# Four graph-attention layers: transposes of features and of layer 1's attention taken from TensorE to VectorE and DRAM

## The chip, the cores and the metric

The kernel runs on one core of a Trainium2 chip. A core has TensorE (PE, matrix products), VectorE (DVE), ScalarE (ACT), GpSimd (POOL) and SyncE (SP), each with a queue of its own that it works off in order, and DMA engines [...]. Here SyncE only issues plain DMAs; GpSimd also issues DMAs that add to what lies at the destination. The metric is the device time of one execution in microseconds, as the median of several runs. A profile belongs to one execution; its span runs from the first instruction to the last.

## What is computed

The input is 128 independent graphs of 128 nodes with 512 features each, all float32, and an integer adjacency matrix per graph. Four layers follow one another, and each adds its result to x:

```python
h = maximum(layernorm(x), 0.0)
x = x + attention_layer(h, adj)     # four different ones
```

Each attention layer forms, for every pair of nodes, a score from one number of the source and one of the destination, passes it through a leaky ReLU, masks it with the adjacency, takes a softmax over the neighbours and averages features with these weights. The layers differ as follows.

- Layer 0: one head; the scores come from h by two vectors that are folded out of the weights; the values are h itself; an ELU at the end.
- Layer 1: two attention layers in a row. The first projects 512 features to 1024 (4 heads of 256), with a bias and an ELU; the second projects 1024 to 512 with one head.
- Layer 2: one head, scores from h by two vectors, values h.
- Layer 3: a projection from 512 to 512 with 8 heads of 64, a ReLU at the end.

## The kernel before

A graph is one tile: its 128 nodes are the 128 partitions, its 512 features lie along the free axis. `graph(b)` runs the four layers for one graph as a Python generator that yields one step at a time. `Scheduler` takes the steps of up to `FLYING` = 10 graphs, estimates for each when its engine, its inputs and its buffers would be free (`Step.estimate` holds the assumed durations), and writes out the one that could start first; ties go by `rank`, which gives each graph a due time. So the order of every engine's queue is fixed when the kernel is built. Buffers come from pools by a tag with a count (`tile_of("ht", 3, ...)`), and a stream waits until one has been given back. Every instruction of the graphs is recorded at one line of the scheduler, L252 in the profile before, and groups are told apart by their tiles.

The parts that the change touches:

- `norm_relu` (mean and variance with `bn_stats` and `bn_aggr` on VectorE, the reciprocal root on GpSimd, the scaled ReLU on ScalarE) makes h. Its columns come from a small pool.
- `transposed` turns 128x128 blocks on TensorE against `ident` into a PSUM bank and copies the bank to SBUF on ScalarE. Layers 1 and 3 need h with features first (`ht`, four blocks), since a product takes its left side with the summed index on the partitions. Layer 1 also turns its four heads of attention weights e (`et`), and the other attentions turn one block each in `attended`.
- `rows_in_dram` takes a few columns, one number per node, turns them on TensorE into rows, copies them on ScalarE to `r` and writes `r` to DRAM. From there they are read back by every partition: into layer 1's e by SyncE, and onto layer 3's `sd` by a GpSimd DMA that adds. The last `LATE` = 5 graphs avoid that for layer 3 and add rows on VectorE from PSUM (`add_rows`).
- `projected` multiplies `ht` with the weights: `w1x` for layer 1 in three parts of 344 columns into `fx` (tag `xl`, two of them), `w2x` for its second half in two parts of 257 columns, `wpx` for layer 3 in two parts of 264.
- In `layer1`, VectorE multiplies e by 1/z before it is turned; after the product with the values, VectorE adds the bias, takes the minimum with 0 over all 1024 columns, ScalarE takes the exponential, and VectorE combines them.
- In `layer3`, two SyncE copies fill `sd` with the mask `m` and its transpose `m3t`, each repeated for 8 heads.
- `setup` loads the weights and folds the attention vectors into them; `load` brings x and adj ahead of use.

float32 products go through TensorE as two records each, a transpose as one.

Of the kernel before, what the change touches and what calls it, by code (L numbers as in the profile page):

```python
# [19 lines left out]
SLOPE = 0.2  # L20
EPS = 1e-5
FLYING = 10
AHEAD = 2
# [19 lines left out]
class Step:  # L43
# [17 lines left out]
    def estimate(self, name, outs, ins, kw):  # L61

        if name == "dma_start":

            rate, busy = (290e3, 0.35) if self.engine == "SP" else (105e3, 1.0)
            self.moves = size(outs[0]) * outs[0].shape[0] * 4 / rate
            return busy, 1.0
        n = max(size(a) for a in outs[:1] + ins)
        if self.engine == "PE":
            if name == "transpose":  # L70
                return 0.109, 0.2
            return 2 * max(0.00084 * size(outs[0]), 0.108), 0.2
        if self.engine == "DVE":
            if name == "bn_stats":
                return 0.6, 0.12
            if name == "bn_aggr":
                return 0.09, 0.12
            per = 1 / 960
            if name == "tensor_scalar" and n >= 256:
                per /= 2  # L80
            return n * per + 0.07, 0.12
        if self.engine == "ACT":
            pointers = sum(isinstance(kw.get(k), bass.AP) for k in ("bias", "scale"))
            busy = n * 0.00081 + 0.105 + (0, 0.075, 0.135)[pointers]
            return busy + 0.1 * ("accum_out" in kw), 0.15
        if self.engine == "POOL":
            if kw.get("op") == ALU.pow or ALU.pow in kw.get("ops", ()):
                return 0.6, 0.1
            return (0.25 if n <= 16 else 0.55 if name == "tensor_scalar" else 1.3), 0.1
        raise ValueError(name)  # L90


class Group(Step):
    def __init__(self, steps):
# [5 lines left out]
        self.delay = steps[-1].delay  # L100

# [34 lines left out]
class Scheduler:  # L136
    def __init__(self):
# [3 lines left out]
        self.moved = 0.0  # L141
# [95 lines left out]
    def issue(self):  # L237
# [17 lines left out]
        if step.moves:  # L255

            self.moved = max(end, self.moved) + step.moves
            end = self.moved + 1.0
# [21 lines left out]
def kernel(  # L280
# [31 lines left out]
    AG = 4 if B % 4 == 0 else 1  # L312

# [44 lines left out]

    w1x = rows_of("w1x", KC, E1 + HF)
# [22 lines left out]

    def setup():
# [12 lines left out]
        for c in range(KC):  # L396
            yield S.dma_start(out=w1x[c][:, E1:], in_=l1_w1[c * P : (c + 1) * P])
# [16 lines left out]
        for c in range(KC):  # L414
            yield S.dma_start(
                out=wpx[c][:, :, E3:],
                in_=l3_wp[c * P : (c + 1) * P].rearrange("p (h k) -> p h k", h=H3),
# [25 lines left out]
    def fold(blocks, vecs, per, to):  # L443
# [4 lines left out]
        for g in range(0, len(blocks), 4):  # L448
# [5 lines left out]
                        lhsT=wt[:, j - g, :],  # L454
# [7 lines left out]
            give_back(wt)  # L462
# [33 lines left out]
    def norm_relu(xt):  # L496

        st6 = column("st6", nc.vector.BN_STATS_DIM)
        yield V.bn_stats(st6, xt)
        mv = column("mv", nc.vector.BN_AGGR_DIM)  # L500
        yield V.bn_aggr(mv, st6)
        ve = column("ve")
        yield G.tensor_scalar(ve, mv[:, 1:2], EPS, None, ALU.add)
        rstd = column("rstd")
        yield G.tensor_tensor(out=rstd, in0=ve, in1=minus_half, op=ALU.pow)
        nmr = column("nmr")
        yield V.scalar_tensor_tensor(nmr, mv[:, 0:1], -1.0, rstd, ALU.mult, ALU.mult)
        h = yield tile_of("h", 4, D)
        yield A.activation(out=h, in_=xt, func=AF.Relu, bias=nmr, scale=rstd)
        return h  # L510
# [18 lines left out]
    def transposed(blocks, tag, bufs):  # L529

        n = len(blocks)
        r = yield tile_of(tag, bufs, n, P)
# [4 lines left out]
        yield A.copy(r.rearrange("p m q -> p (m q)"), pt[:, : n * P])  # L537
        give_back(pt)
        return r

    def rows_in_dram(cols, n):

        r = yield Take(work, [2 * H3, P], "r", 4)
        r = r[:n]
        pt = yield bank()
        yield T.transpose(pt[:n, :P], cols, ident)
        yield A.copy(r, pt[:n, :P])
        give_back(pt)
        d = dram.tile([n, P], F32, tag=f"d{n}", name="d")
        yield S.dma_start(out=d, in_=r)  # L550
        give_back(r)
        return d.rearrange("n q -> (n q)").partition_broadcast(P)

    def spread(cols, n, to):

        d = yield from rows_in_dram(cols, n)
        yield S.dma_start(out=to, in_=d)
# [19 lines left out]
    def added(cols, to, late, rows=None):  # L577
# [4 lines left out]
        if rows is None:  # L582
            rows = yield from rows_in_dram(cols, cols.shape[1])
        yield G.dma_start(out=to, in_=rows, accum_op=ALU.add)

    def attention(own, rows, e, mask, nh, exact=False):

        mx = column(f"mx{nh}", nh)  # L590
# [3 lines left out]
                    out=e[:, j, :],  # L594
# [11 lines left out]
        if rows[0].tensor.name != e.tensor.name:  # L606
            give_back(rows[0])
# [6 lines left out]
        if exact:  # L614
            ef = e.rearrange("p h q -> p (h q)")
            yield V.tensor_scalar(ef, ef, own, None, ALU.add)
            yield V.scalar_tensor_tensor(ef, ef, SLOPE, ef, ALU.mult, ALU.max)
        else:
            for j in range(nh):
                yield A.activation(  # L620
                    out=e[:, j, :],
                    in_=e[:, j, :],
# [4 lines left out]
        for j in range(nh):  # L627
            yield A.activation(
                out=e[:, j, :],
                in_=e[:, j, :],  # L630
# [8 lines left out]
    def attended(own, other, mask, values, exact=False):  # L639

        e = yield tile_of("e0", 3, 1, P)
        pb = yield bank()
        yield T.transpose(pb[:, :P], other.to_broadcast([P, P]), ident)
        rz = yield from attention(own, [pb[:, :P]], e, mask, 1, exact)
        et = yield from transposed([e[:, 0, :]], "et0", 3)
        give_back(e)
        pa = yield bank()
        yield T.matmul(pa, lhsT=et[:, 0, :], rhs=values, start=True, stop=True)
# [3 lines left out]
    def projected(lhs, n_k, w, parts, to, beside=None, plus=None):  # L652
# [4 lines left out]
        for i in range(parts):  # L657
            lo = i * width
            pm = yield bank()
            for g in range(0, n_k, 4):  # L660
# [4 lines left out]
                            lhsT=lhs[:, c, :],  # L665
# [41 lines left out]
    def layer1(xt, mask):  # L707
        h = yield from norm_relu(xt)
        ht = yield from transposed(blocks_of(h), "ht", 3)
        give_back(h)  # L710
        yield Until("w1")
        fx = yield tile_of("xl", 2, E1 + HF)
        e = yield tile_of("e1", 3, H1, P)
        rows = e.rearrange("p h q -> p (h q)")
        fork = yield from projected(
            ht, KC, w1x, 3, columns(fx, 3), lambda: spread(fx[:, :H1], H1, rows)
        )
        give_back(ht)
        xl = fx[:, E1:]
        yield Join(fork)  # L720
        rz = yield from attention(fx[:, H1:E1], [e[:, j, :] for j in range(H1)], e, mask, H1)
        yield V.tensor_tensor(e, e, rz.unsqueeze(2).to_broadcast([P, H1, P]), ALU.mult)
        et = yield from transposed([e[:, j, :] for j in range(H1)], "et1", 3)
        give_back(e)
        y = yield tile_of("y1", 2, FC, P)
        for g in range(0, FC, 4):
# [6 lines left out]
                        rhs=et[:, c * P // F1, :],  # L733
# [5 lines left out]
            )  # L739
            yield V.tensor_tensor(  # L740
                y[:, g : g + 4, :],
# [5 lines left out]
        give_back(fx, et)  # L747
        yf = y.rearrange("p c q -> p (c q)")

        t = yield tile_of("t1", 1, HF)  # L750
        yield V.tensor_scalar(t, yf, 0.0, None, ALU.min)
        yield A.activation(out=t, in_=t, func=AF.Exp)
        yield V.scalar_tensor_tensor(yf, t, -1.0, yf, ALU.add, ALU.max)
        give_back(t)
# [3 lines left out]
        yield from projected(y, FC, w2x, 2, columns(gx, 2), plus=columns(b2, 2))  # L758
# [18 lines left out]
    def layer3(xt, mask, mask_t, late):  # L777
# [3 lines left out]
        ht = yield from transposed(blocks_of(h), "ht", 3)  # L781
# [8 lines left out]
        for to, m in (d, mask), (e, mask_t):  # L790
            yield S.dma_start(out=to, in_=m.unsqueeze(1).to_broadcast([P, H3, P]))
            give_back(m)
# [8 lines left out]
        give_back(ht)  # L801
# [12 lines left out]
        fork = None if late else (yield Fork(rows_in_dram(mx, H3)))  # L814
# [60 lines left out]
    def graph(b):  # L875
# [9 lines left out]
        m3t = yield tile_of("m3t", FLYING, P)  # L885
        m1 = yield tile_of("m1", FLYING, P)
# [6 lines left out]
        yield from layer1(xt, m1)  # L893
# [7 lines left out]
        yield from layer3(xt, m3, m3t, b >= B - LATE)  # L901
# [65 lines left out]
```

## Time and profile before

| What | Before |
|---|---|
| Median of three runs | 3410.93 us (3409.13 to 3411.11) |
| The profiled execution | 3414.4 us |
| Its span | 3412.6 us |
| Mean granted TensorE clock | 0.991 |
| VectorE busy | 2617.3 us, 77% |
| ScalarE busy | 2316.5 us, 68% |
| GpSimd busy | 871.6 us, 26% |
| Moved by DMA | 450.33 MB, mean 132 GB/s |

A line of a group reads: line of the code, engine, operation, output<-inputs by tile name (buffer numbers left out), shape, count; then busy time and mean duration of one in ns; then how long the engine was idle just before such instructions, and what ended most of that. Busy time of an engine counts overlapping instructions once, so the groups of an engine whose instructions overlap add up to more than its total. `PEld` is TensorE's loading of weights, which overlaps its products. `SPq` and `POOLq` are the queues that issue DMAs; issuing isn't counted as busy.

### The profile page before, as it was taken

How to read it: one execution, taken by the hardware profiler on the slowest of the kernel's cores; microseconds unless marked ns; L12 is line 12 of the kernel's file. 1: busy time of each engine (PE TensorE's matmuls, PEld its weight loads, DVE VectorE, ACT ScalarE, POOL GpSimd, SP SyncE). 2: the span in 40 equal slices, each digit the busy share in tenths (PEclk: the TensorE clock that was granted, in tenths of full speed). 3: DMA queues.
4: the chain of work that ended last, by engine and by line, in shares of the span. 5: the costliest groups of instructions: out<-in, count | busy, mean ns of one | idle time of the engine just before them, and what ended most of it. 6: DMA issues, size and time to landing. Idle time of an engine off the chain costs nothing.

```text
span 3412.6 us, 56516 instructions
## 1 busy us (share of the span) xinstructions
PE 3381.6 (99%) x17118; PEld 2650.2 (78%) x17118; DVE 2617.3 (77%) x9296; ACT 2316.5 (68%) x6661; POOL 871.6 (26%) x1791
## 2 busy tenths in 40 slices
PE   8999999999999999999999999999999999999998
PEld 5777777777777777777777777777777777777787
DVE  6777777777778777777777787777787777777766
ACT  4667676677677667666767766776776676667764
POOL 1222322222222222222222222222222222222221
PEclk7999999999999999999999999999999999999998
DMA  5155555555556556555655555565565555556553
GB/s 151 45 125 127 139 139 132 131 142 138 131 126 151 129 132 145 132 128 140 143 130 132 133 144 133 138 142 128 123 151 134 134 138 135 131 131 143 131 126 97
DMA packets 392879, 450.33 MB, mean 132 GB/s; under 512 B 27128, under 2 KB 309120, under 8 KB 376832
## 3 DMA queue, kind: packets, MB, share of 16 engines
q0 software_dynamic: 35424, 193.48, 29.3%
q1 hardware_dynamic: 352976, 253.23, 25.4%
q8 instruction: 137, 2.24, 0.3%
q14 instruction: 166, 1.36, 0.1%
q10 hardware_dynamic: 4176, 0.02, 0.1%
HBM read 277.11 MB, written 35.33 MB: 92 GB/s over the span
## 4 chain that ended last, share of the span: by engine, by line
PE 98%; ACT 1%; DVE 1%; issue 0%; DMA 0%; POOL 0%; ACTq 0%; POOLq 0%; DVEq 0%
PE bank L252 98%; DVE sd L252 0%; ACT ht L252 0%; DMA a<-in_L_gnn_a_dram 0%; ACT h L252 0%; ACT sd L252 0%; ACT e L252 0%; DMA at<-in_adj_dram 0%; POOL rstd L252 0%; DVE st L252 0%; DVE products L252 0%; DVE xt L252 0%; DVE e L252 0%; POOL ve L252 0%; DVE mx L252 0%
## 5 line engine op out<-in xcount | busy, mean ns | idle before, releaser
L252 PE MATMUL bank<-w2x,y 128*128 128x257 f32 x4096 | 975.2, 381 | 0.0
L252 PE MATMUL bank<-w1x,ht 128*128 128x344 f32 x3072 | 954.3, 454 | 1.4 <-ACT ht L252 1.4
L252 PEld LDWEIGHTS bank<-w2x,y 128*128 128x128 f32 x4096 | 746.8, 190 | 108.3 <-issue 16.7
L252 PEld LDWEIGHTS bank<-w1x,ht 128*128 128x128 f32 x3072 | 572.2, 191 | 261.1 <-issue 17.9
L252 ACT ACTIVATE h<-xt,nmr,rstd 128x512 f32<-128x512 f32 x512 | 413.6, 808 | 386.1 <-DVE nmr L252 385.0
L252 PE MATMUL bank<-wpx,ht 128*128 128x264 f32 x2048 | 501.9, 388 | 0.0
L252 POOL TENSOR_SCALAR ve<-mv 128x1 f32<-128x1 f32 x512 | 173.5, 339 | 1095.1 <-DVE mv L252 905.5
L252 PEld LDWEIGHTS bank<-wpx,ht 128*128 128x128 f32 x2048 | 381.1, 191 | 87.4 <-DVE y L252 8.6
L252 ACT ACTIVATE sd<-sd,f 128x128 f32<-128x128 f32 x1024 | 366.2, 392 | 0.0
L252 ACT ACTIVATE e<-e,nm 128x128 f32<-128x128 f32 x896 | 351.4, 396 | 13.8 <-DVE e L252 9.5
L252 DVE BATCH_NORM_STATS2 st<-xt 128x6 f32<-128x512 f32 x512 | 350.7, 685 | 0.0
L252 POOL TENSOR_TENSOR rstd<-ve,minus_half 128x1 f32<-128x1 f32 x512 | 313.7, 613 | 42.0
L252 PEld LDWEIGHTS bank<-x,sd 128*128 128x128 f32 x2048 | 266.1, 194 | 48.2 <-issue 12.2
L252 POOL DMA_DIRECT2D sd<-d x246 | 230.7, 994 | 267.5 <-ACT sd L252 136.7
L252 PEld LDWEIGHTS bank<-et,xl 128*128 128x128 f32 x2048 | 250.3, 192 | 38.4 <-issue 37.5
L252 PE MATMUL bank<-et,xl 128*128 128x128 f32 x2048 | 271.8, 276 | 0.2 <-ACT et L252 0.2
L252 PE MATMUL bank<-x,sd 128*128 128x65 f32 x2048 | 260.1, 271 | 7.2 <-ACT sd L252 7.2
L252 PE MATMUL bank<-h,et 128*128 128x512 f32 x512 | 266.1, 601 | 0.7 <-ACT et L252 0.7
L252 ACT COPY xl<-bank 128x344 f32<-128x344 f32 x384 | 166.7, 434 | 135.0 <-PE bank L252 134.6
L252 DVE TENSOR_TENSOR y<-bank,b 128x512 f32<-128x512 f32 x256 | 176.8, 690 | 81.4 <-PE bank L252 72.9
L252 ACT COPY x<-bank 128x264 f32<-128x264 f32 x256 | 96.0, 375 | 210.1 <-PE bank L252 209.9
L252 DVE SCALAR_TENSOR_TENSOR xt<-bank,rz,xt 128x512 f32<-128x512 f32 x256 | 191.3, 747 | 23.6 <-PE bank L252 23.5
(90 smaller groups left out, 5207.0 us busy)
## 6 DMA issues: line engine op xcount, KB each, us to landing
sd<-d POOLq DMA_DIRECT2D x123, 1024.0 KB, 11.0
sd<-m SPq DMA_DIRECT2D x128, 512.0 KB
sd<-m3t SPq DMA_DIRECT2D x128, 512.0 KB
sd<-d POOLq DMA_DIRECT2D x123, 512.0 KB, 8.3
xt<-in_x_dram SPq DMA_DIRECT2D x128, 256.0 KB
e<-d SPq DMA_DIRECT2D x128, 256.0 KB
out_dram<-xt SPq DMA_DIRECT2D x128, 256.0 KB
at<-in_adj_dram SPq DMA_DIRECT2D x32, 256.0 KB
```

Of the source, the lines that this page charges most:

```text
L252: method(*args, **kw)
```

## The change

Features first without TensorE: `turned` transposes a 128x512 tile on VectorE in place, as 32x32 squares (each square within its 32 partitions and 32 columns), writes it to DRAM in four DMAs, one for each group of 32 partitions, with pieces of 512 bytes, and reads it back in one DMA with 2 KB per partition, so that squares come to the partitions where they belong. For h the columns are dealt: feature (q, k) of the 512 stands at 4q + k, so block k takes every fourth column of `ht`, and the rows of `w1x` and `wpx` are loaded in the same order (`dealt`). For layer 1's e the squares are contiguous; e is laid out with the heads inside groups of 32 columns. The last five graphs (`late`) still use TensorE, with dealt columns.

`rows_in_dram` now turns a 128x32 tile of repeated columns on VectorE and writes it to DRAM in four DMAs, or for layer 1 (`together`) in one, from which e is read with 512-byte pieces.

Layer 1's scaling by 1/z moves from VectorE to ScalarE, one instruction per head. Its ELU goes by halves of 512 columns, with ScalarE's ReLU of -y in place of VectorE's minimum. `m3t` is stored in DRAM in between and is read from there. `norm_relu` keeps its columns in one tile of a pool of six. There are three `xl` tiles, two `et1`, two half-sized `t1`, seven `m1`; `FLYING` is 12, `AHEAD` 1, and the scheduler's DMA estimates are changed, with a separate clock for each issuing queue.

```diff
-FLYING = 10
-AHEAD = 2
+FLYING = 12
+AHEAD = 1
 LATE = 5
...
-            rate, busy = (290e3, 0.35) if self.engine == "SP" else (105e3, 1.0)
+            rate, busy, delay = (280e3, 0.4, 0.5) if self.engine == "SP" else (150e3, 1.0, 2.0)
+            if self.engine == "SP" and max(len(a.shape) for a in outs + ins) > 2:
+                busy = 0.65
...
+    Q = nc.vector.STREAM_SQUARE_SIZE
+    R = P // Q
...
+    def dealt(w):
+        return w.rearrange("(p c) n -> c p n", c=KC)
...
-            yield S.dma_start(out=w1x[c][:, E1:], in_=l1_w1[c * P : (c + 1) * P])
+            yield S.dma_start(out=w1x[c][:, E1:], in_=dealt(l1_w1)[c])
...
+    def turned(t, squares, tag, bufs):
+        yield V.transpose(squares, squares)
+        f = t.shape[1] // R
+        d = dram.tile([R, Q, R, f], F32, tag="turned", name="turned")
+        yield Group(
+            [
+                S.dma_start(
+                    out=d[:, :, r].rearrange("m b f -> b m f"),
+                    in_=t[r * Q : (r + 1) * Q].rearrange("b (m f) -> b m f", m=R),
+                )
+                for r in range(R)
+            ]
+        )
+        to = yield tile_of(tag, bufs, R * f)
+        yield S.dma_start(out=to, in_=d.rearrange("m b r f -> (m b) (r f)"))
+        return to
+
+    def features_first(h, late):
+        if late:
+            blocks = h.rearrange("p (q k) -> p k q", k=KC)
+            return (yield from transposed([blocks[:, k] for k in range(KC)], "ht", 3, True))
+        to = yield from turned(h, h.rearrange("p (m b k) -> p m k b", b=Q, k=KC), "ht", 3)
+        blocks = to.rearrange("p (q k) -> p k q", k=KC)
+        return [blocks[:, k] for k in range(KC)]
+
+    def rows_in_dram(cols, n, together=False):
+        r = yield tile_of("r", 5, Q)
+        yield V.transpose(r, cols)
+        if together:
+            d = dram.tile([R, Q, Q], F32, tag="squares", name="d")
+            yield S.dma_start(out=d.rearrange("c m b -> (c m) b"), in_=r)
+            give_back(r)
+            rows = d[:, :n].rearrange("c m b -> c (m b)")
+            return rows.unsqueeze(0).to_broadcast([P, R, n * Q])
+        d = dram.tile([n, R, Q], F32, tag=f"d{n}", name="d")
+        yield Group(
+            [S.dma_start(out=d[:, c], in_=r[c * Q : c * Q + n]) for c in range(R)]
+        )
         give_back(r)
...
-        ht = yield from transposed(blocks_of(h), "ht", 3)
+        ht = yield from features_first(h, late)
...
-        fx = yield tile_of("xl", 2, E1 + HF)
+        fx = yield tile_of("xl", 3, E1 + HF)
...
-        yield V.tensor_tensor(e, e, rz.unsqueeze(2).to_broadcast([P, H1, P]), ALU.mult)
-        et = yield from transposed([e[:, j, :] for j in range(H1)], "et1", 3)
+        for j in range(H1):
+            yield A.activation(out=heads[j], in_=heads[j], func=AF.Copy, scale=rz[:, j : j + 1])
+        if late:
+            et = yield from transposed(blocks_of(e), "et1", 2)
+        else:
+            to = yield from turned(e, e, "et1", 2)
...
-        t = yield tile_of("t1", 1, HF)
-        yield V.tensor_scalar(t, yf, 0.0, None, ALU.min)
-        yield A.activation(out=t, in_=t, func=AF.Exp)
-        yield V.scalar_tensor_tensor(yf, t, -1.0, yf, ALU.add, ALU.max)
+            t = yield tile_of("t1", 2, 4 * P)
+            yield A.activation(out=t, in_=yg, func=AF.Relu, scale=-1.0)
+            yield A.activation(out=t, in_=t, func=AF.Exp, scale=-1.0)
+            yield V.scalar_tensor_tensor(yg, t, -1.0, yg, ALU.add, ALU.max)
...
+        m3t_far = dram.tile([P, P], F32, tag="m3t", name="m3t_far")
+        yield S.dma_start(out=m3t_far, in_=m3t)
+        give_back(m3t)
+        yield from layer1(xt, m1, b >= B - LATE)
```

## The prediction

> **What bounds the kernel now.** The median is 3410.93 us (3409.13 to 3411.11). The profiled execution took 3414.4 us, 3412.6 of them span, so sums made against the span become a median by adding 1.8 and taking off 3.5. I read busy shares first, then the chain that ended last, then TensorE's groups with shapes kept apart.
>
> ```profile
> PE 3381.6 (99%) x17118; PEld 2650.2 (78%) x17118; DVE 2617.3 (77%) x9296; ACT 2316.5 (68%) x6661; POOL 871.6 (26%) x1791
> ...
> q0 software_dynamic: 35424, 193.48, 29.3%
> q1 hardware_dynamic: 352976, 253.23, 25.4%
> ...
> PE 98%; ACT 1%; DVE 1%; issue 0%; DMA 0%; POOL 0%; ACTq 0%; POOLq 0%; DVEq 0%
> ```
>
> TensorE is both 99% busy and 98% of the chain. In the windows its idle time lies at the ends: 15.5 us in the first 80 us, some 14 in the last 72, about 1 us in the others I read. Only removing TensorE work can shorten this kernel, and only while nothing else takes over. The five groups that the change touches:
>
> ```profile
> L252 PE MATMUL bank<-ident,e 128*128 128x128 f32 x896 | 175.6, 274 | 4.8 <-ACT e L252 4.8
> L252 PE MATMUL bank<-ident,h 128*128 128x128 f32 x1024 | 154.7, 274 | 1.1 <-ACT h L252 1.1
> ...
> L252 PE MATMUL bank<-ident,xl 128*4 128x128 f32 x128 | 34.9, 272 | 0.0
> L252 PE MATMUL bank<-ident,f 128*16 128x128 f32 x123 | 33.5, 273 | 0.0
> L252 PE MATMUL bank<-ident,mx 128*8 128x128 f32 x123 | 33.5, 272 | 0.0
> ```
>
> The 274 ns are a duration, not a price: matmuls overlap. The timeline (start, duration) gives the price as start to start:
>
> ```profile
> 1718.57 0.60 PE L252 MATMUL bank<-ident,h 128*128 128x128 f32 x4
> 1719.00 0.27 PE L252 MATMUL bank<-ident,mx 128*8 128x128 f32 x1
> 1719.11 0.74 PE L252 MATMUL bank<-w1x,ht 128*128 128x344 f32 x2
> ```
>
> Four transposes take 0.43 us and one 0.11, so 0.109 us each, narrow or full. The same reading over 800 us gives 0.289 per 344-column matmul and 0.222 per 264-column one.
>
> The last view is SyncE's own queue. The 1 MB of mask copies fills something: the issue behind them takes 6.52 us instead of its usual 0.36.
>
> ```profile
> 1747.40 0.60 SPq L252 DMA_DIRECT2D sd<-m  x1
> 1748.06 0.95 SPq L252 DMA_DIRECT2D sd<-m3t  x1
> 1749.10 6.52 SPq L252 DMA_DIRECT2D out_dram<-xt  x1
> 1755.66 1.22 SPq L252 DMA_DIRECT2D xt<-in_x_dram  x1
> ```
>
> Before, this hits about one graph in four; the others leave the queue empty for some 13 us after the mask copies.
>
> [...] 128x512 should then cost what other one-element passes cost, 686 ns in this trace; no transpose runs before. [...] The new weight blocks step exactly four; nothing in the trace strides so[...]. [...] SyncE's issue above stalls while POOL's two accumulations also run.
>
> **The change, part by part.**
>
> *TensorE.* The order of instructions, changed against before: transposes of h 1024 to 40, of e 896 to 404, of xl 128 to 0, of f (16 columns) 123 to 0, of mx (8 columns) 123 to 0. That is 1850 fewer, 15 per graph in 123 graphs (the last five keep those of h and layer 1's e). 1850 x 0.109 = 202 us. Nothing is added; other matmuls keep their shapes.
>
> *VectorE.* Removed: e times rz (87.8), the min on y (88.2), the 1024-wide combine (155.9): 332 us. Added: 369 transposes of 128x512 at 0.686 = 253; 256 half-width combines at 0.686 = 176; 374 transposes of 128x32 at about 0.17 (between the one-column rows, 0.153, and 128x128, 0.28) = 64. Net +161, so 2778 us. If stride-4 access halved the 246 transposes of h, +169 more. 85% to 90% of 3268 us: hidden by TensorE, with a thin cover.
>
> *ScalarE.* Removed: 254 contiguous copies to ht net of the new dealt ones (145), 123 to et (71), 374 row copies (93), the 1024-wide exp (135). Added: 512 scalings at 0.392 (the row with one pointer) = 201, and 512 half-width relu and exp at about 0.67 (between 0.39 for 128 and 1.06 for 1024) = 343. Net +100, 2417 us, 74%: covered. POOL keeps its 1796 instructions; the statistics in one tile instead of columns cost nothing but a place of six.
>
> *DMA engines.* Before: 55% of 3412.6 = 1884 us. The hardware queue pays 25.4% of the span for 253.23 MB, 3.42 us per MB. Each of 369 turns writes and reads 0.262 MB: 193.5 MB = 662 us. Parking m3t adds 8.4 MB, 29 us. So 2575 us, 79%. The pieces are 512 bytes written and 2 KB read, around the queue's 717-byte mean; I keep the mean.
>
> *SyncE's queue.* 1076 issues become 3802, 30 per graph. Twelve turning writes at 0.33 (bounds 0.25, a small row copy, and 0.65, the mask copy) = 4.0; three reads at 0.36 = 1.1; nine small row copies 2.5; e 0.45 (as adj, of its shape); two mask copies 1.27; m3t out 0.35; out, xt, a quarter adj 0.9; 30 gaps of 0.08 = 2.4. Sum 12.9 us per graph, before about 4. Behind the mask copies come now always four row copies, m3t and two turns, so I charge the stall to every graph: 7 us. A read that follows its writes by four issues waits for them: 1 to 2 us each, 3 in all (POOL's wait for d shows about 1.5 from issue to landing). Total 23 us, bounds 17 (stall covered by the wait for f, which the queue has anyway) and 28 (0.65 per write, 5 of waits). What stands behind a blocked SyncE is everything: rows for POOL's additions, et and ht for TensorE, x for the next graph.
>
> *Pace.* In the steady stretch the mask copies come every 25.95 us on average. TensorE will need 25.95 - 1.64 = 24.3. SyncE's 23 lie just under it. VectorE, 2778/128 = 21.7; DMA, 20.1. Four queues within 20% of each other, in one order fixed beforehand, won't mesh as before, when TensorE waited 6 us in 3230. I charge 0.35 us per graph, 45 us (between nothing and 1.64, the whole gain). *Ends:* the first features go through DRAM while weights load (DMA share 0.95 and 1.06 in the first two 20 us windows): +15 us (0 to 30). The last five graphs keep the old path. Twelve graphs and three projection tiles cover latency: a turn adds some 6 us, three per graph 18, while two more graphs give 2 x 24.3 of time. They save nothing alone.
>
> 3412.6 - 202 + 45 + 15 = 3270.6 span, +1.8 - 3.5 = 3269 us.
>
> **Rivals.** *(B) SyncE sets the pace, a part of the gain stays.* For it: 23 us with bounds 17 and 28 around 24.3. Against: the stall partly falls where the queue waits for f anyway. Between 25.0 and 25.9 per graph: 3330 to 3404, say 3370.
>
> *(C) The same queue ends slower.* From 25.95 us per graph on, nothing is left. At 27.0, which writes at 0.65 would give: 3412.6 + 123 x 1.05 + 15 = 3557 span, 3555 us. For it: the 6.52 us line. Against: SyncE's other issues are short, and DMA's own work is 20.1.
>
> *(D) Strided weights.* Loads of 128 columns follow each other at 0.11 (et,xl: matmuls start every 0.111 with one load each). At twice that, 0.22, they hide under 0.289 and 0.222. It decides from 0.222 on; at 0.33, 3072 x 0.041 + 2048 x 0.108 = 347 us, 3410.9 + 347 - 202 = 3556 us or more. [...]
>
> *(E) VectorE takes over.* It idles 795 us now, largely waiting on TensorE, ScalarE and POOL in its order. If 500 of these stay on 2778, 3280; with the doubled transposes 3450. The middle is about 3340. *(F) The stalls don't come:* 3225.
>
> **How the numbers follow.** A, the forecast with F inside it, 3205 to 3330: 0.50. B 0.20. C 0.15. D 0.07. E 0.08, half of it above no change. A measurement here can tell about 0.2%, 7 us. Faster: A, B less 0.02, half of E = 0.72. Same: 0.03 from B's and C's edges. Slower 0.25. The likeliest case's own range is 3205 to 3330. The range 3205 to 3500 leaves out a few per cent below and D and the larger part of C above, under 0.2 together.
>
> **What would show it.** Right: TensorE's transposes at 40 and 404, no row transposes, TensorE busy near 3180 at 96% or more of the span; VectorE 83 to 88%; DMA share near 0.8; TensorE's waits mostly for ht, et and e, each by a DMA. F: waits below 20 us. B or C: TensorE below 95%, SyncE's issues behind the mask copies at several us in every graph, TensorE and VectorE waiting for DMA reads. D: wpx matmuls starting more than 0.23 apart without a wait. E: VectorE above 92% and on the chain. Wrong for a cause I don't list: small DMA waits, but TensorE idle behind POOL's accumulations.

## The result and the profile after

The changed kernel takes 3930.62 us as the median of four runs (3918.25 to 3933.85), the kernel before 3410.72 (3409.13 to 3411.11). The ratio is 1.1519, with a 95% interval of 1.1493 to 1.1544: 520 us slower, where I had forecast 142 faster. The time lies outside my range, and far above the 3555 us of rival C.

The profiled execution took 3928.6 us, 3926.8 of them span. Its page answers the lines shown of before as follows (busy times, DMA queues, chain by engine; every step now stands at line 255):

```profile
PE 3494.9 (89%) x15268; PEld 2940.1 (75%) x15268; DVE 2767.7 (70%) x9911; ACT 2370.5 (60%) x6814; POOL 786.9 (20%) x1791
...
q1 hardware_dynamic: 718880, 457.01, 41.1%
q0 software_dynamic: 35424, 193.48, 26.9%
...
PE 41%; DMA 28%; DVE 11%; issue 9%; POOL 5%; SPq 3%; ACT 2%; POOLq 0%; DVEq 0%; ACTq 0%
```

TensorE has 1850 fewer instructions and yet more busy time than before, 3494.9 us against 3381.6, and 432 us of the span in which it is idle, against 31. The chain, which was TensorE for 98%, is TensorE for 41% and DMA for 28%. So two things are to be explained: some 315 us of busy time beyond the 3180 that I had worked out, and some 400 us more of idle time than before.

The transposes are gone as planned, by the same list of TensorE's groups with shapes kept apart:

```profile
L255 PE MATMUL bank<-ident,e 128*128 128x128 f32 x404 | 110.0, 280 | 12.1 <-ACT e L255 12.1
...
L255 PE MATMUL bank<-ident,h 128*128 128x128 f32 x40 | 6.7, 290 | 0.3 <-ACT h L255 0.2
```

The page's costliest groups show where the time came. First three lines of the page before, to compare with:

```profile
L252 PEld LDWEIGHTS bank<-w1x,ht 128*128 128x128 f32 x3072 | 572.2, 191 | 261.1 <-issue 17.9
...
L252 POOL DMA_DIRECT2D sd<-d x246 | 230.7, 994 | 267.5 <-ACT sd L252 136.7
...
L252 PE MATMUL bank<-x,sd 128*128 128x65 f32 x2048 | 260.1, 271 | 7.2 <-ACT sd L252 7.2
```

And after:

```profile
L255 PE MATMUL bank<-w1x,ht 128*128 128x344 f32 x3072 | 1135.8, 519 | 6.8 <-DMA ht<-turned 6.8
L255 PEld LDWEIGHTS bank<-w1x,ht 128*128 128x128 f32 x3072 | 895.5, 315 | 120.0 <-issue 98.1
...
L255 PE MATMUL bank<-x,sd 128*128 128x65 f32 x2048 | 314.2, 305 | 336.3 <-issue 328.6
...
L255 POOL DMA_DIRECT2D sd<-d x246 | 234.7, 956 | 1493.6 <-DMA d<-r 1117.8
...
L255 DVE STREAM_TRANSPOSE h<-h 128x512 f32<-128x512 f32 x246 | 276.1, 1122 | 10.7 <-ACT h L255 10.4
```

The turned features are nearly always there in time: TensorE waits 6.8 us in the whole span for `ht<-turned` ahead of w1x. Of its 432 idle us, 336.3 stand before the products `x,sd`, layer 3's last (before: 7.2), nearly all put down to "issue", that is to nothing that the profile shows as a wait. GpSimd stands 1117.8 us before its accumulations `sd<-d`, waiting for the rows that SyncE writes (`d<-r`). Loading a weight block of `ht` takes 315 ns, where it took 191, and the transposes of h take 1122 ns each.

The timeline of one graph's layer 3 (start, duration, engine, operation; in brackets the idle time before it) shows how these belong together:

```profile
1719.91 1.22 DVE L255 TENSOR_REDUCE mx<-sd 128x8 f32<-128x1024 f32 x1 [1.46 <-DMA sd<-d]
...
1722.13 0.21 DVE L255 STREAM_TRANSPOSE r<-mx 128x32 f32<-128x32 f32 x1
...
1722.84 2.11 SPq L255 DMA_DIRECT2D turned<-e  x4
...
1726.56 2.18 SPq L255 DMA_DIRECT2D d<-r  x4
...
1730.29 0.94 POOL L255 DMA_DIRECT2D sd<-d  x1 [6.93 <-DMA d<-r]
...
1730.99 0.55 POOL L255 TENSOR_TENSOR f<-x,b_l 128x16 f32<-128x16 f32 x1
...
1731.81 5.14 SPq L255 DMA_DIRECT2D d<-r  x4
...
1737.35 1.06 ACT L255 ACTIVATE sd<-sd 128x1024 f32<-128x1024 f32 x1 [1.07 <-DMA sd<-d]
...
1738.51 1.08 PE L255 MATMUL bank<-x,sd 128*128 128x65 f32 x8 [3.13 <-issue]
1739.42 4.26 PE L255 MATMUL bank<-w1x,ht 128*128 128x344 f32 x8
...
1740.68 0.97 POOL L255 DMA_DIRECT2D sd<-d  x1 [5.06 <-DMA d<-r]
```

The first accumulation has landed and VectorE takes its maximum at 1719.91. The row r is ready at 1722.34, but SyncE comes to write it only at 1726.56, after the four writes of e and 1.6 us more. The second accumulation starts at 1730.29 and has landed at 1737.35, when ScalarE's exponential can start. It ends at 1738.41, and 0.1 us later TensorE starts on `x,sd`: the "issue" wait of 3.13 us is the wait for this exponential. Meanwhile the next graph's rows (1731.81) stand 5.14 us in SyncE's queue behind the mask copies of 1730.20 and 1730.84, and GpSimd's next first accumulation starts at 1740.68. The one before it in the trace had started at 1711.38, so this graph takes 29.3 us; over 80 graphs in the middle of the trace it is 30.1 on average, against 25.95 before.

The lines also show why these waits add up to the time of a graph. GpSimd makes the next graph's `f` (1730.99), from which the rows of its first accumulation come, only behind the second accumulation of this graph, by 0.7 us in the median. So the two round trips through SyncE and DRAM come one after the other: 19.2 us from first to second accumulation and 10.8 from there to the next first (medians), together the 30 us of a graph. In the kernel before, the next `f` was made ahead of the second accumulation, by 4.3 us in the median, and the two accumulations were issued side by side (`x2`):

```profile
1743.10 0.25 POOL L252 TENSOR_TENSOR f<-x,b_l 128x16 f32<-128x16 f32 x1
...
1745.20 1.90 POOL L252 DMA_DIRECT2D sd<-d  x2 [1.85 <-ACT ht L252]
```

And here pauses of TensorE are followed by a slower clock. The windows view (stretch, its length, busy us of PE, PEld, DVE, ACT and POOL with the number of instructions, granted clock, DMA share, GB/s) of the same stretch:

```profile
1735.00:1740.00 5.00, 1.87 (x11) 1.51 (x11) 3.38 (x15) 3.93 (x10) 0.62 (x2) 0.95 0.76 190
1740.00:1745.00 5.00, 5.00 (x19) 3.64 (x18) 4.49 (x11) 2.88 (x7) 1.99 (x4) 0.71 0.56 105
```

After the pause of 3.13 us the granted clock falls to 0.71 over five microseconds, and the eight products of 1739.42 take 4.26 us; the next eight, at 1744.48, take 2.59.

The clock records of the whole trace, without 100 us at either end, bear this out. They hold 78 stretches at half clock, of 3.4, 6.8 or 10.2 us, and each begins in a pause of TensorE or within 4 us after one. All 62 pauses of 3 us or more have such a stretch, 16 of the 28 pauses between 1.5 and 3 us, and none of the 50 between 0.5 and 1.5. The mean clock of the run is 0.934, before 0.991, so (1 - 0.934) x 3926.8 = 259 us of clock are lost, where (1 - 0.991) x 3412.6 = 31 were. By the same records 215 of the lost us, before 24, fall into TensorE's busy time: some 190 of its 315 us. My prediction had not asked what a pause would do to the clock.

### The profile page after: what moved, and what is told of

Same layout as the page of the kernel before. It is cut to its first block, busy times and chain, and to the rows that moved or that the text cites. A ratio compares the mean times of both kernels' runs of the same rounds, so it can differ in the third digit from the quotient of the medians.

```text
span 3926.8 us, 57931 instructions
## 1 busy us (share of the span) xinstructions
PE 3494.9 (89%) x15268; PEld 2940.1 (75%) x15268; DVE 2767.7 (70%) x9911; ACT 2370.5 (60%) x6814; POOL 786.9 (20%) x1791
## 4 chain that ended last, share of the span: by engine, by line
PE 41%; DMA 28%; DVE 11%; issue 9%; POOL 5%; SPq 3%; ACT 2%; POOLq 0%; DVEq 0%; ACTq 0%
PE bank L255 41%; DMA d<-r 9%; DMA sd<-d 8%; DMA ht<-turned 7%; SPq L255 3%; DVE st L255 3%; DMA e<-d 3%; POOL sd L255 2%; DVE xt L255 2%; POOL st L255 2%; DVE mx L255 1%; DVE m L255 1%; DVE y L255 1%; DVE h L255 1%; DMA sd<-m3t_far 1%
## 5 line engine op out<-in xcount | busy, mean ns | idle before, releaser
L255 PE MATMUL bank<-w1x,ht 128*128 128x344 f32 x3072 | 1135.8, 519 | 6.8 <-DMA ht<-turned 6.8
L255 PEld LDWEIGHTS bank<-w1x,ht 128*128 128x128 f32 x3072 | 895.5, 315 | 120.0 <-issue 98.1
L255 PE MATMUL bank<-x,sd 128*128 128x65 f32 x2048 | 314.2, 305 | 336.3 <-issue 328.6
L255 POOL DMA_DIRECT2D sd<-d x246 | 234.7, 956 | 1493.6 <-DMA d<-r 1117.8
L255 PEld LDWEIGHTS bank<-wpx,ht 128*128 128x128 f32 x2048 | 499.3, 323 | 34.4 <-issue 7.8
L255 ACT ACTIVATE h<-xt,st 128x512 f32<-128x512 f32 x512 | 406.5, 805 | 187.3 <-DVE st L255 183.4
L255 POOL TENSOR_SCALAR st<-st 128x1 f32<-128x1 f32 x512 | 154.5, 310 | 1299.6 <-DVE neg L255 754.7
L255 POOL TENSOR_TENSOR st<-st,minus_half 128x1 f32<-128x1 f32 x512 | 293.8, 578 | 23.0
L255 DVE STREAM_TRANSPOSE h<-h 128x512 f32<-128x512 f32 x246 | 276.1, 1122 | 10.7 <-ACT h L255 10.4
L255 DVE TENSOR_REDUCE mx<-sd 128x8 f32<-128x1024 f32 x128 | 155.8, 1217 | 169.2 <-DMA sd<-d 167.0
L255 DVE SCALAR_TENSOR_TENSOR y<-t,y 128x512 f32<-128x512 f32 x256 | 176.1, 688 | 127.5 <-ACT t L255 127.1
```

What stands on the lines that cost most here:

```text
L255: method(*args, **kw)
```

## The experiments

All are single executions beside one run of the kernel before on the same chip (3406.6 to 3415.1 us), so I read nothing into differences of less than 20 us. Nearly every variant is also planned anew, and a new plan alone moved the changed kernel by 39 us one way and 230 the other (below). So a piece of some tens of us is what a variant costs together with its new order. In the expectations, L and L2 stand for round trips through SyncE and DRAM that the engines wait for, S for the strided weight blocks, Q for the load on queues and DMA engines, F for the frame around the transposes, P for the plan's estimates, H for TensorE's waiting on h, W for the work of turning h.

### Parts taken back from the changed kernel

*Mask copies issued by ScalarE's queue*, so that rows do not stand behind them.

```diff
+    S2 = Engine("SP", nc.scalar)
...
-            yield S.dma_start(out=to, in_=m.unsqueeze(1).to_broadcast([P, H3, P]))
+            yield S2.dma_start(out=to, in_=m.unsqueeze(1).to_broadcast([P, H3, P]))
```

> The changed kernel, with layer 3's two mask copies issued from ScalarE's queue in place of SyncE's; the plan is the same. Theory L (a loop of 29.3 us per graph: rows of f behind the mask copies on SyncE, first accumulation, maximum, rows of mx, second accumulation, and through GpSimd's queue the next graph's f): the four row copies behind the masks take 2.3 us in place of 5.1 and land 1 to 2 us sooner, so the loop becomes 24.5 to 26.5 us and the time 3330 to 3550. Theory S (strided weight loads are the main loss): unchanged, 3900 to 3950. Theory Q (SyncE simply has too many issues, 30 per graph): two of 30 less, 3800 to 3900.

Measured: 3881.6 us, in Q's range and far above L's, with TensorE's order unchanged. The timeline of this kernel, GpSimd's accumulations and the row writes ahead of one:

```profile
1702.48 0.97 POOL L255 DMA_DIRECT2D sd<-d  x1 [4.07 <-DMA d<-r]
...
1724.88 0.94 POOL L255 DMA_DIRECT2D sd<-d  x1 [11.11 <-DMA d<-r]
1726.40 1.99 SPq L255 DMA_DIRECT2D d<-r  x4
1730.89 0.97 POOL L255 DMA_DIRECT2D sd<-d  x1 [0.68 <-DMA d<-r]
...
1759.94 0.97 POOL L255 DMA_DIRECT2D sd<-d  x1 [4.02 <-DMA d<-r]
```

The stall is gone (1.99 us for four writes instead of 5.14), and from the second accumulation to the next first one only 6.0 us pass instead of 10.4. But from first to second it is now 22.4 us instead of 18.9, and a graph still takes 28.4 to 29.1. The wait moved along the loop. The stall behind the mask copies is worth some 49 us, not the 520.

*Layer 3's rows back on TensorE*: one transpose, a copy on ScalarE and one DMA instead of a VectorE transpose and four.

```diff
-            rows = yield from rows_in_dram(repeated(cols), cols.shape[1])
+            rows = yield from rows_by_pe(cols, cols.shape[1])
...
-        fork = None if late else (yield Fork(rows_in_dram(repeated(mx), H3)))
+        fork = None if late else (yield Fork(rows_by_pe(mx, H3)))
```

> The changed kernel, with layer 3's rows (f and mx) turned on TensorE again and written to DRAM by one DMA each in place of four. TensorE gets 2 x 123 x 0.109 = 27 us more. Theory L: each row copy costs the loop 0.3 us in place of 2.2 and about 3 in place of 5.1, with a hop over TensorE and ScalarE of 1 us each added: 26 to 28 us per graph, 3500 to 3750. Theory S: 3930 + 27, about 3950. Theory Q: 24 issues in place of 30, up to a fifth less: 3300 to 3500.

Measured: 3783.2 us, 147 less and outside all three ranges, although TensorE has 246 transposes more (27 us). TensorE is busy for 91%.

*h back on TensorE* with contiguous blocks and plainly loaded weights, in all graphs.

```diff
-            return (yield from transposed([blocks[:, k] for k in range(KC)], "ht", 3, True))
-        to = yield from turned(h, h.rearrange("p (m b k) -> p m k b", b=Q, k=KC), "ht", 3)
...
+        return (yield from transposed(blocks_of(h), "ht", 3))
```

> The changed kernel, with h turned on TensorE again in layers 1 and 3 in every graph and plain weight order; e and the rows stay on VectorE and DRAM. 984 transposes come back, 107 us of TensorE, the stride of 115 us goes, SyncE has 10 issues less per graph, DMA 129 MB less. Theory L: the row copies still stand behind the mask copies, the loop is shorter only by less company on the DMA engines: 3500 to 3750. Theory Q or the DMA load: back to 3300 to 3430.

Measured: 3662.3 us, 268 less, with 984 transposes (107 us) more; L's range holds it.

*Both of these*, so that only layer 1's e and its row go by VectorE and DRAM.

> The changed kernel with h and layer 3's rows back on TensorE and plain weights; left of the transposes on VectorE are layer 1's e (four writes, one read) and its row. TensorE saves 123 x 5 x 0.109 = 67 us against the kernel before. Theory L2 (not one block but the whole round trip of the row copies and accumulations on one fixed order, lengthened by every added DMA): with five DMAs per graph more than before, in place of 22, most of the loss goes, 3380 to 3500. If losses simply add (h 268, rows 147): 3930 - 415 = 3515. Theory F (the frame: twelve graphs, the other DMA estimates, m3t by way of DRAM): still above 3600.

Measured: 3508.4 us, 422 less, where the two alone add up to 416: the two costs are separate to within the noise, as the expectation's simple sum of 3515 had it.

*Only the frame*: e back as well, so that TensorE transposes all that it did before. What is left of the change are twelve graphs, the pools, ScalarE's scaling, the ELU by halves, `m3t` by way of DRAM and the scheduler's DMA estimates.

> The changed kernel with every transpose back on TensorE: of the change there remain twelve graphs in flight, three projection tiles, the DMA estimates of the plan, m3t by way of DRAM, the scaling on ScalarE and the ELU by halves. TensorE's work is that of before. Theory L2: close to before, 3400 to 3450. Theory F: above 3500.

Measured: 3546.3 us. The frame alone costs 137, as F had it. TensorE's wait for `sd`, ahead of layer 3's last products, is 96.6 us in this kernel, where it was 7.2 before, although no transpose has moved. And e through VectorE gives 38 us back, while it takes 68 us (492 and 128 transposes by 0.109) from TensorE.

### The stride alone

The kernel before, with ScalarE's copy dealing the columns of `ht` so that a weight block takes every fourth; nothing else moves.

```diff
-        yield A.copy(r.rearrange("p m q -> p (m q)"), pt[:, : n * P])
+        yield A.copy(r, pt[:, : n * P].rearrange("p (m q) -> p m q", m=n))
```

> The kernel before, with ht alone laid out so that each block's columns lie four apart: the transposes stay on TensorE, ScalarE's copy writes strided. Theory S by the starts in the changed kernel (0.305 against 0.289 per w1x product, 0.254 against 0.222 per wpx product): 3072 x 0.016 + 2048 x 0.032 = 115 us, 3500 to 3550. If the loads cost nothing of themselves and the longer starts come from the pauses: 3405 to 3430. If they are the main loss: above 3700.

Measured: 3470.0 us, 58.6 more. Its groups with shapes kept apart:

```profile
L252 PEld LDWEIGHTS bank<-w1x,ht 128*128 128x128 f32 x3072 | 875.7, 311 | 25.2 <-PE bank L252 7.4 <-ACT ht L252 3.3 <-issue 2.0
...
L252 PE MATMUL bank<-wpx,ht 128*128 128x264 f32 x2048 | 535.9, 405 | 0.0
```

A load takes 311 ns where it took 191. Added up from each start to the next over the whole run, the products over w1x take 912.6 us instead of 891.8 and those over wpx 494.6 instead of 460.5, 55 us more together (0.007 and 0.017 us per product). That is between the two ranges expected. The 0.254 per wpx product of the expectation, and with it the 115 us, was read with pauses behind the products in it; without these the median there is 0.248. TensorE stays 99% busy at a clock of 0.992, so this is the price of the stride with nothing else waiting, and S explains about a ninth of the loss.

### The plan

*The changed kernel, planned with the DMA estimates of before* (one clock for all queues, 290 and 105 GB/s).

```diff
-            rate, busy, delay = (280e3, 0.4, 0.5) if self.engine == "SP" else (150e3, 1.0, 2.0)
-            if self.engine == "SP" and max(len(a.shape) for a in outs + ins) > 2:
-                busy = 0.65
+            rate, busy, delay = (290e3, 0.35, 1.0) if self.engine == "SP" else (105e3, 1.0, 1.0)
...
-            end = max(end, self.moved.get(step.engine, 0.0)) + step.moves
-            self.moved[step.engine] = end
-            end += 0.4
+            end = max(end, self.moved.get("all", 0.0)) + step.moves
+            self.moved["all"] = end
+            end += 1.0
```

> The changed kernel, planned with the DMA estimates of the kernel before (290 and 105 GB/s on one common clock, 0.35 us per SyncE issue). All instructions stay, their order changes. Theory P (the order is made for latencies that the chip doesn't keep, since the two queues are planned as if each had the DMA engines for itself): the order allows longer for the additions, 3450 to 3700. Theory L2 with the added DMAs themselves as the price: 3850 to 4000.

Measured: 3969.7 us, 39 more; P falls in this form.

*The same, planned with estimates nearer to what the trace shows*: one clock for all queues, 280 and 183 GB/s, 0.5 us per SyncE issue, 1.5 us to land, the products over `ht` 1.05 and 1.14 times as long, the transposes of h 1.8 times.

> The changed kernel, planned with estimates from its own trace: one common DMA clock, 280 and 183 GB/s, 0.5 us per SyncE issue, 1.5 us to land, strided products 5% and 14% longer, the strided transpose 1.8 times as long. Theory P: the pauses of TensorE before layer 3's last products mostly go, 3350 to 3600. Theory L2: 3800 to 4000.

Measured: 3700.1 us, 230 less, with not one instruction added or removed. TensorE's idle time falls from 432 to 301 us and its busy time from 3494.9 to 3397.4. Neither theory had this: the order is worth 230 us, and yet 290 stay.

*The frame with the DMA estimates of before.*

> All transposes on TensorE and the frame of the change, planned with the DMA estimates of the kernel before (one common clock, 290 and 105 GB/s). Theory P (the new estimates let layer 3's last products come too early; 137 us in the frame are theirs): 3405 to 3440. If twelve graphs, the moved scaling or m3t by way of DRAM cost it: 3520 to 3560.

Measured: 3423.3 us. Of the frame's 137 us, 123 are the changed DMA estimates, and TensorE's wait for `sd` is back at 9.0 us: P holds for the frame. Twelve graphs, smaller tiles and the shifted work cost about nothing, nor do they gain. The page's busy times and chain:

```profile
PE 3386.2 (99%) x17118; PEld 2647.4 (77%) x17118; DVE 2426.3 (71%) x9168; ACT 2616.6 (76%) x7557; POOL 855.9 (25%) x1791
...
PE 96%; DVE 1%; ACT 1%; issue 1%; DMA 1%; POOL 0%; SPq 0%; POOLq 0%; ACTq 0%; DVEq 0%
```

*The same plan with e through VectorE and DRAM.*

> Only layer 1's e and its row through VectorE and DRAM, h and layer 3's rows on TensorE, planned with the DMA estimates of the kernel before. TensorE has 67 us less to do than before. Theory P: 3345 to 3390, faster than both kernels. If five more DMAs per graph cost more than they save whatever the plan: 3420 to 3520.

Measured: 3413.2 us, beside 3415.1 of before: no difference, and neither theory's range. TensorE has 48 us less busy time than with the frame (3338.1), but the time is only 10 us shorter, which is too little to count.

*All cures together*: the nearer estimates, layer 3's rows on TensorE, mask copies from ScalarE's queue.

> The changed kernel with three cures at once: planned with estimates from its own trace, layer 3's rows back on TensorE by one DMA each, mask copies on ScalarE's queue; h and e still through VectorE and DRAM. If the cures add up (230 of 3930 for the plan, 147 for the rows, 49 for the masks): 3500. If they treat the same wait and it is gone with the first two: 3450 to 3600, with TensorE's pauses before layer 3's last products under 50 us and the rest in strided products. If the turning of h itself is the bound, by its two hops through DRAM: above 3620.

Measured: 3774.5 us, slower than the nearer estimates alone. The cures do not add; each also changes the order in which the rest is laid out. The time lies where the expectation had put the turning of h as the bound, so h comes next. In a stretch after a 2.82 us pause, eight products over `y` took 3.63 us instead of 1.90, so the slowed clock isn't a matter of strided blocks.

### h taken apart

These stand on the frame with the DMA estimates of before (3423 us), where order and latencies did no harm.

*h alone through VectorE and DRAM.*

> The frame planned with the DMA estimates of before (3423 us) with only h turned through VectorE and DRAM in 123 graphs; e and all rows stay on TensorE. TensorE loses 984 transposes x 0.109 = 107 us, the strided blocks alone cost 59. Theory P (the changed estimates in the plan did the harm): 3423 - 107 + 59 = 3375, range 3350 to 3420. Theory H (the round trip is waited for whatever the plan): 268 more than without it, as in after, less what the plan has of it: 3520 to 3690. Theory W (the work on VectorE, SyncE and the DMA engines, in whatever order): the same as f_shadow less about 107.

Measured: 3650.4 us, 227 more and in H's range. P falls for this part: on a plan that was good for all else, turning h costs nearly what it cost in the changed kernel (268).

*The same work unused*: TensorE turns h itself, into strided blocks, as the last five graphs do. Beside it VectorE turns h, and the writes and the read go on, but nothing takes the result.

```diff
+    def shadow(h):
+        yield from turned(h, h.rearrange("p (m b k) -> p m k b", b=Q, k=KC), "hs", 2, h)
+        give_back(h)
...
+        ht = yield from transposed([blocks[:, k] for k in range(KC)], "ht", 3, True)
...
+            yield Fork(shadow(h))
```

> The same frame with h transposed on TensorE into strided blocks, as the last five graphs have it, and beside it the turn of h on VectorE, the four writes and the read back into h, whose result nobody takes. It saves TensorE nothing, and carries all the work and the stride of f_h without TensorE waiting for it. Theory H and theory P: only the stride, 3423 + 59 = 3482, range 3470 to 3510. Theory W: 3423 + 59 plus what the work costs, above 3540.

Measured: 4485.1 us. This is a fault of the experiment: it keeps each h until the unused read has landed, and there are only four h tiles. It says nothing on work against waiting. So both were repeated with six h tiles, and two `xl` tiles to make room.

> f_h with six h tiles and two xl tiles. The h pool is not what binds f_h (h is given back when its writes have landed), so about as f_h: 3650, range 3600 to 3700. If it falls below 3550, the pool of h was the cause.

Measured: 3576.8 us, 74 below f_h and outside what I expected: the pool of h was part of the cost of turning h, since a turned h is held until its writes have landed. TensorE's wait for `ht<-turned` falls from 40.4 to 3.6 us. Its page:

```profile
PE 3421.5 (96%) x16134; PEld 2964.1 (83%) x16134; DVE 2692.1 (75%) x9414; ACT 2517.8 (70%) x7311; POOL 855.0 (24%) x1791
...
L253 PE MATMUL bank<-w1x,ht 128*128 128x344 f32 x3072 | 1005.9, 472 | 0.3 <-DMA ht<-turned 0.3
```

> The same six and two. TensorE turns h itself into strided blocks and waits for nothing of the turn that goes on beside it. Theory H (TensorE's wait for the round trip costs): only the stride and ScalarE's slower copy on the frame's 3423, so 3470 to 3530. Theory W (the work of the turn costs, on VectorE, SyncE and the DMA engines): f_h6's time plus up to 107, 3650 to 3800.

Measured: 3681.3 us, 104 above f_h6. Its page:

```profile
PE 3526.6 (96%) x17118; PEld 3085.7 (84%) x17118; DVE 2682.6 (73%) x9414; ACT 2712.0 (74%) x7557; POOL 901.8 (25%) x1791
```

TensorE is 105 us busier than in f_h6, and idle for as long: 153 us of the span here, 154 there. So most of what TensorE saves by the turn is saved: 984 x 0.109 = 107 us at the price of before, and 123 at the price of this kernel, whose transposes read every fourth column and start 0.121 us apart or more. TensorE hardly waits for the round trip, and the same idle time stands in a kernel that takes nothing from it. With six h tiles H falls, and W holds, as far as it means all that the turn brings along. Three more take that apart: no unused turn at all, VectorE's transposes alone, the DMAs alone.

> f_shadow6 without the unused turn: h on TensorE into strided blocks in every graph, on the planned frame with six h and two xl tiles. If the stride costs here what it cost in b_strided: 3423 + 59 = 3482, range 3460 to 3510. Above 3560 the strided blocks, with ScalarE's slower copy, are the larger part of the 258 us.

> The unused turn's VectorE transposes alone, no DMA. If VectorE's work in its fixed order is the cost: 3640 to 3690. If the DMAs are: as f_shadow_0 within 30 us.

> The unused turn's DMAs alone (h written out as it is and read back), no VectorE transpose. If SyncE's queue and the DMA engines are the cost: 3640 to 3690. If VectorE is: as f_shadow_0 within 30 us. If the two costs add up: f_shadow_v and this one together exceed f_shadow_0 by the 199 of f_shadow6.

Measured: 3579.5, 3617.8 and 3662.1 us. VectorE's transposes cost 38 us and the ten DMAs per graph 83; together they cost 102 (3681 less 3580), so they nearly add, and the DMAs are the larger part. Three limits: 38 us lies between the two ranges expected; each has its own order; and in the run with the DMAs each h is held until its unused read has landed. ScalarE's direct waits ahead of an h are small there, under 10 us for all DMAs; what the holding does to the order was not separated.

TensorE's share falls from 98% to 97%, 96% and 96%, and no other engine is above 75%. The products themselves do not get slower: whole groups of eight over w1x start 0.304 us apart per product, in the median, in all four. Of the 83 us of the DMAs, 52 are idle time of TensorE. Its wait for `sd`, ahead of layer 3's last products, grows from 7.6 to 39.6 us, and the granted clock falls from 0.992 to 0.981.

The 156 us from the frame (3423) to f_shadow_0 are more than the 59 of the stride alone. ScalarE's slower copy to `ht` stands in both, 1061 ns instead of 572 in the kernel with the stride alone, where TensorE stayed 99% busy beside it. In f_shadow_0 the transposes of h also read every fourth column, which makes TensorE 11 us longer, and 41 us of its idle time wait for ScalarE's `et` and `e`. How the other 98 divide between the copy, that reading, the changed pools (six h tiles, two `xl` tiles) and the order was not told apart.

## Why the prediction was wrong

*TensorE's transposes* were right in their counts (1850 less, 40 and 404 left) and in their price: added up from start to start they take 200 us less than before, for 202. But the sum also took the price of all other products as fixed ("Nothing is added; other matmuls keep their shapes"). That price rose, by some 55 us for the stride and some 190 for the clock.

*VectorE, ScalarE, DMA engines.* The totals were close: 2768 us measured for 2778, 2371 for 2417, and 68.4% of 3926.8 = 2686 us for 2575. The transposes of h took 1122 ns, where I had 686 as the likeliest and a doubling as the other bound; the e transposes, without the stride, took 691. Both bounds were estimates: 686 ns is what other passes over 128x512 took in the trace before, and what a stride would cost was not shown there. Here the stride did cost: TensorE's loads went from 191 to 311 ns and ScalarE's copy to `ht` from 572 to 1061 (the kernel with the stride alone), and VectorE's transpose takes 1122 with the stride and 691 without.

*Rival D* I had dismissed with loads that double to 0.22 and hide under products of 0.222, an estimate from the 0.111 per load of the trace before. They do hide for the most part, but products over wpx start 0.017 later on average and those over w1x 0.007: 59 us in the kernel with the stride alone, between the nothing that I took and the 347 of the rival's other end. The sign that I had named for D, wpx more than 0.23 apart without a wait, came true (0.248) at a sixth of that price.

*SyncE's queue* was described rightly in the main: in 91 of 128 graphs four row writes stand right behind the mask copies and take 5.2 us in the median (put at 7), and the four writes of a turn take 2.4 us (put at 1.3). I had named these as a sign of B and C. (B's sum was wrong: by C's formula its 25.0 to 25.9 us per graph make 3309 to 3420, not 3330 to 3404.) But SyncE's issues fill only 18 of the 30 us of a graph, so its sum was not what set the pace.

*Pace* is the step that failed: "I charge 0.35 us per graph, 45 us". It took each queue as a sum to be compared with TensorE's 24.3 us, and "twelve graphs and three projection tiles cover latency" as the answer to everything else. What took the place of it is 30.1 us per graph, so 5.8 us instead of 0.35 beyond the 24.3 that I had counted for TensorE: some 2.5 of its work grown dearer and some 3.3 of its pauses. They come from these parts, in the order in which they were taken back (frame +137, e -38, layer 3's rows +154, h +268, sum 521):

- The order. It is fixed when the kernel is built, from estimates of DMA times. With the changed ones, 123 us are lost before anything is moved; with nearer ones, 230 are won back at once. My prediction saw that the estimates were changed and gave that no cost. That the estimates of before are good for the frame and bad for the whole (3970) shows that they are no recipe either.
- Layer 3's rows: from TensorE and one write to VectorE and four writes behind others. Maximum, row, second accumulation, exponential and `x,sd` follow one another, 18.6 us in the timeline shown. From the maximum to the exponential it is no longer than before (17.9 us in the median of both), but the next graph's `f` and first accumulation now come behind it and not beside it, and TensorE's queue has the products in a fixed place, so it pauses. I had counted the row's parts in each queue and never laid the two round trips of a graph end to end.
- Pauses of TensorE: all 62 of 3 us or more, and 16 of the 28 between 1.5 and 3 us, come with a stretch at half clock. That is a part of why its busy time rose with less work: of the 315 us beyond 3180, some 190 are lost clock by the trace's records and some 55 the stride by the kernel with the stride alone; the other 70 were not assigned.
- h: stride, the DMAs, VectorE's longer transposes and the h tiles that are held longer. I had looked at the pools that were resized, and not at the one, of h with four tiles, in which each tile is now held longer. On the frame, six tiles instead of four, with two `xl` tiles, gave 74 us.

The line on being "wrong for a cause I don't list: small DMA waits, but TensorE idle behind POOL's accumulations" comes closest to what the trace shows: 14.7 us of TensorE waits for `ht<-turned`, and its idle time behind the exponential of the second accumulation. It stood there as a sign only, without a cost.

What stays open: how h's 268 us in the changed kernel divide, since the pieces were measured on another plan, and the 98 us named above. Turning h without a stride was not tried. No version beat both kernels by more than a single run can tell; the nearest, e alone on the plan of before, equals it.

## What to carry to other kernels

TensorE was 99% busy here, and with 6% of its work taken away (200 of 3382 us) the kernel lost 520 us: with what took the work over, TensorE was idle for 432 us, where it had been for 31. So lay the moved steps end to end, through every queue, landing and consumer, before adding each queue up by itself. DMA estimates in the plan that didn't hold cost 123 us in the frame and 230 in the whole, so plan again with durations from a trace and test the frame of a change alone. And ask of every pool, not only of those that were resized, how long its tiles are now held.

## What the runs showed of the hardware

- In the changed kernel each of 62 pauses of TensorE of 3 us or more comes with a stretch at half clock, of 3.4, 6.8 or 10.2 us, as do 16 of 28 pauses between 1.5 and 3 us and none of 50 between 0.5 and 1.5 us. In the one shown, eight products over w1x take 4.26 us instead of 2.59.
- float32 at a stride of four elements: in the kernel with the stride alone weight loads took 311 ns instead of 191 and a 128x512 ScalarE copy from PSUM 1061 instead of 572; in the changed kernel a 128x512 VectorE transpose took 1122 (h) instead of 691 (e). The loads were mostly hidden behind the products, 59 us in 5120 of them. TensorE's transposes of h started 0.121 us apart where they read at that stride, instead of 0.109.
- Unused DMAs beside TensorE did not slow its products as such: over strided blocks they started 0.304 us apart, in the median of groups of eight, with and without them. The kernel with the DMAs was 83 us longer, by TensorE's waits and the clock.
- An issue on SyncE behind 1 MB of mask copies took 5.14 us for four small writes; issued from ScalarE's queue, the copies left them at 1.99. The kernel gained 49 us of the 520 by it; no run here tells issue time from transfer time.
